# Layer 0 of a two-layer attention kernel: transposes in step 3 and in score tiles, other products at the ends of steps, moments over two steps

## The chip, the cores and the metric

The kernel runs on one core of one Trainium2 chip. A core has five engines that run side by side, each working through its own list of instructions in order, and telling each other of progress through semaphores: TensorE (PE; its weight loads are listed apart as PEld), VectorE (DVE), ScalarE (ACT), GpSimd (POOL) and SyncE (SP), which here issues all DMA transfers. PE writes its results to PSUM, DVE and ACT take them from there to SBUF, the working memory[...].

The metric is the device time of one execution in microseconds (us), lower is better. Before the change it was 3759.24 us, the median of three runs (3758.98 to 3764.71).

## The reference

The input x has 128 rows (S) of 256 positions (I) with 256 channels (C), all in float32. Two residual layers follow each other, each with a group norm in front:

```python
# layer 0: attention over the positions of a row, 8 heads of 32 channels, pair bias, gate
m_norm = layer_norm(m, ln_m_w, ln_m_b)          # m = _gn(x)
q = (m_norm @ Wq.T); k = (m_norm @ Wk.T); v = (m_norm @ Wv.T)      # split into 8 heads
b = (layer_norm(z) @ Wb.T)                       # a bias for each head, position and position
gate = sigmoid(m @ Wg.T + bg)
p = softmax(q @ k.T / sqrt(32) + b)
x = x + ((p @ v) * gate) @ Wo.T + bo
# layer 1: attention with 4 heads of 64 channels within a band of 16 positions
q, k, v = split(_gn(x) @ w_in.T + b_in)
x = x + softmax(band(q @ k.T / sqrt(64))) @ v @ w_out.T + b_out
```

Only the order of work in layer 0 is touched by the change; what is computed stays the same.

## The kernel before

The kernel has a part ahead of layer 0 (it makes the exponentials of the pair bias, `eb`, and the group moments of x), layer 0 and layer 1. Rows are worked on in pairs (class `Pair`); there are 64 pairs (`NP`), and a pair's input tile `xt` holds two rows as four blocks of 128 positions (`NT` = 4, `NB` = 2 blocks a row), 512 positions in all (`N2`). Channels are cut into two chunks of 128 (`KC` = 2).

For a pair, these methods run in turn. `Pair()` loads `xt` by DMA. `centre` and `scale` (POOL) make the group-normed `xg`. `moments` (DVE) gives each position's variance: four `bn_stats`, four `bn_aggr` and an addition. `root` raises it to the power -1/2 on POOL, and then two DMAs bring it from one value for each partition (`lrs`) to a row that stands in every partition: L1188 writes `rs_d` in memory, L1190 reads it back as `rs_r`, 128 copies of 512 values. `residual` (POOL) adds the output bias to `xt`. `turn` transposes `xg` on PE, four blocks for each chunk; of each result DVE makes `xnT`, multiplied with `rs_r` (L1200), and ACT the plain copy `xgT` (L1201). `project` makes qT and kT from `xnT` and gT from `xgT`, one chunk at a time; ACT takes the result from PSUM. `values(r)` and `keep_values(r)` make v of row r on PE and take it over with DVE.

Then there are four half steps of attention, for row r and chunk c (four heads): `scores(r, c)` on PE into two PSUM tiles, exponentials on ACT; `add_bias` multiplies one half with `eb` on DVE, the other on POOL; one step later `apply` multiplies the exponentials with v and with ones; `invert` takes reciprocals of the sums (DVE), `gate` multiplies with the gate (DVE, two instructions); `out_row` and `keep_row` multiply with Wo and add to the residual. `some(n)` issues up to n of the small DVE instructions that gather the moments for layer 1.

The order is written out by hand (`tc.manual_schedule()`): every engine's list follows the order of the calls. Each pair is four steps, each beginning with a call of `scores`, and in them stands work of four pairs: `was` (the one before), `now`, `nxt` (the next) and `nn` (the one after it). In each step PE's list begins with `scores` and `apply`; what comes after them on PE is:

| Step | scores | PE after scores and apply, before the change | after the change |
|---|---|---|---|
| 1 | now (0,0) | qT 1, kT 1, values 0 | qT 1, kT 1, values 0 |
| 2 | now (0,1) | gT 0, out_row 1 of was | gT 0, out_row 1 of was |
| 3 | now (1,0) | gT 1, values 1 | gT 1, turn of nxt, values 1 |
| 4 | now (1,1) | turn of nxt, out_row 0, qT 0 and kT 0 of nxt | qT 0 and kT 0 of nxt, out_row 0 |

[...] Layer 0 divides them into three pools: `ps_mm`, two tiles of one bank (tag `mm`: transposes, projections, values, output products), `ps_s`, two tiles of two banks (tag `s`: scores; one call of `scores` takes both), and `ps_o`, two tiles of one bank (results of `apply`). A tile is handed out again when its last reader is done. `xgT` and `xnT` have one buffer each in SBUF (`bufs=1`); a tile without `bufs` in the pool `sb` has two.

Of the kernel before, what the change touches and what calls it, by code (L numbers as in the profile page):

```python
# [9 lines left out]
F32 = mybir.dt.float32  # L10
AF = mybir.ActivationFunctionType
ALU = mybir.AluOpType
# [4 lines left out]
P = 128  # L17
# [756 lines left out]
def fast_kernel(  # L774
# [25 lines left out]
    nc = tc.nc  # L800
# [7 lines left out]
    NB = I // P  # L808
    KC = C // P
    NP = S // 2  # L810
    N2 = 2 * I
# [7 lines left out]
    ident = const.tile([P, P], F32, name="ident")  # L819
# [157 lines left out]
    with tc.tile_pool(name="pre", bufs=2) as pre, tc.tile_pool(  # L977
        name="pre1", bufs=1
# [5 lines left out]
        for w, dst in ((wq, qb), (wk, kb)):  # L984
            for m in range(KC):
                ps = pps.tile([P, 512], F32, name="b_ps", tag="mm")
# [7 lines left out]
        ps = pps.tile([P, 512], F32, name="b_ps", tag="mm")  # L994
# [5 lines left out]
        ps = pps.tile([P, 512], F32, name="b_ps", tag="mm")  # L1000
# [9 lines left out]
        for w in (wq, wk, wv):  # L1010
            ps = pps.tile([P, 512], F32, name="b_ps", tag="mm")
# [11 lines left out]
        ps = pps.tile([P, 512], F32, name="b_ps", tag="mm")  # L1023
# [117 lines left out]
    NT = 2 * NB  # L1141
# [5 lines left out]
    with tc.tile_pool(name="l0", bufs=2) as sb, tc.tile_pool(  # L1147
        name="l0s", bufs=4
    ) as sm, tc.tile_pool(name="ps_mm", bufs=2, space=PSUM) as ps_mm, tc.tile_pool(
        name="ps_s", bufs=2, space=PSUM  # L1150
    ) as ps_s, tc.tile_pool(name="ps_o", bufs=2, space=PSUM) as ps_o:

        def mm(name):
            return ps_mm.tile([P, 512], F32, name=name, tag="mm")

        class Pair:
# [15 lines left out]
            def residual(self):  # L1172
                nc.gpsimd.tensor_tensor(self.xt, self.xt, bcast(bo_r, 1, NT), ALU.add)

            def moments(self):
                st = sm.tile([P, NT, 6], F32, name="lst", tag="lst")
                self.mv = sm.tile([P, NT, 2], F32, name="lmv", tag="lmv")
                for t in range(NT):
                    nc.vector.bn_stats(st[:, t, :], self.xg[:, t, :])
                for t in range(NT):  # L1180
                    nc.vector.bn_aggr(self.mv[:, t, :], st[:, t, :])
                self.rs = sm.tile([P, NT], F32, name="lrs", tag="lrs")
                nc.vector.tensor_scalar_add(self.rs, self.mv[:, :, 1], 1e-5)

# [7 lines left out]

            def turn(self):
                self.xgT = sb.tile([P, KC, N2], F32, name="xgT", tag="xgT", bufs=1)
                self.xnT = sb.tile([P, KC, N2], F32, name="xnT", tag="xnT", bufs=1)
                for k in range(KC):
                    ps = mm("ps_x")
                    for t in range(NT):
                        nc.tensor.transpose(ps[:, t * P : (t + 1) * P], self.xg[:, t, k * P : (k + 1) * P], ident)
                    nc.vector.tensor_tensor(self.xnT[:, k, :], ps, self.rs_r, ALU.mult)  # L1200
                    nc.scalar.copy(self.xgT[:, k, :], ps)  # L1201

            def project(self, which, m):
                w, src, b, fn, sc = {
# [145 lines left out]
        def some(n):  # L1350
            for _ in range(min(n, len(later))):
                later.pop(0)()
# [10 lines left out]
        def pair(p):  # L1363
            return Pair(p) if p < NP else Nobody()

        now, nxt, nn = pair(0), pair(1), pair(2)
        for d in (now, nxt):
            d.centre()
            d.scale()
            if d is now:  # L1370
                d.moments()
                d.root()
            d.residual()
        now.turn()
# [3 lines left out]
        with tc.manual_schedule():  # L1378
            was, es, nn3 = Nobody(), None, None
            for p in range(NP):  # L1380

                e = now.scores(0, 0)
                now.add_bias(0, 0, e)
                nn.centre()
                was.apply(1, 1, es)
                was.invert(1, 1)
                was.gate(1, 1)
                now.project("qT", 1)
                now.project("kT", 1)
                nxt.moments()  # L1390
                some(1)
                now.values(0)
                now.keep_values(0)
                es = e

                nxt.root()
                e = now.scores(0, 1)
                now.add_bias(0, 1, e)
                nn.scale()
                now.apply(0, 0, es)  # L1400
                now.invert(0, 0)
                now.project("gT", 0)
                was.out_row(1)
                some(1)
                was.keep_row(1)
                now.gate(0, 0)
                es = e

                nn3 = pair(p + 3)
                e = now.scores(1, 0)  # L1410
                now.add_bias(1, 0, e)
                nn.residual()
                now.apply(0, 1, es)
                now.invert(0, 1)
                now.project("gT", 1)
                some(1)
                now.values(1)
                now.keep_values(1)
                now.gate(0, 1)
                es = e  # L1420

                e = now.scores(1, 1)
                now.add_bias(1, 1, e)
                now.apply(1, 0, es)
                nxt.turn()
                now.invert(1, 0)
                now.out_row(0)
                now.keep_row(0)
                now.gate(1, 0)
                nxt.project("qT", 0)  # L1430
                nxt.project("kT", 0)
                some(2)
                es = e
                was, now, nxt, nn = now, nxt, nn, nn3
            was.apply(1, 1, es)
            was.invert(1, 1)
            was.gate(1, 1)
            was.out_row(1)
            was.keep_row(1)
            some(len(later))  # L1440
# [26 lines left out]
    with tc.tile_pool(name="l1", bufs=2) as sb, tc.tile_pool(  # L1467
        name="l1s", bufs=4
    ) as sm, tc.tile_pool(name="ps1_mm", bufs=2, space=PSUM) as ps_mm, tc.tile_pool(
        name="ps1_s", bufs=1, space=PSUM  # L1470
    ) as ps_s, tc.tile_pool(name="ps1_o", bufs=1, space=PSUM) as ps_o:

        def mm1(name):
            return ps_mm.tile([P, 512], F32, name=name, tag="mm")
# [4 lines left out]
        for k in range(KC):  # L1479
            ps = mm1("ps_mr")  # L1480
# [137 lines left out]
        d = {}  # L1618
        for _ in prep1(0, d):
            pass  # L1620
        for p in range(NP):
            nxt = {}
# [16 lines left out]
            d = nxt  # L1639
# [5 lines left out]
    with tc.tile_pool(name="chk", bufs=1) as ck, tc.tile_pool(name="chk_ps", bufs=1, space=PSUM) as cps:  # L1645
        check(eb.rearrange("p h b i -> p (h b i)"), math.exp(-20.0), math.exp(20.0), 0, ck)
        for j, src in enumerate((rsum.rearrange("n q r c i -> (n q r c i)"), rsum1.rearrange("n q r i -> (n q r i)"))):
            t = ck.tile([P, src.shape[0] // P], F32, name=f"rs_all{j}")
            nc.sync.dma_start(t, src.rearrange("(a b) -> a b", a=P))
            check(t, 1e-16, 1e8, 1 + j, ck)  # L1650
        t = ck.tile([S, I], F32, name="mask_all")
# [4 lines left out]
        ps = cps.tile([P, 512], F32, name="ok_ps")  # L1656
# [4 lines left out]
@with_exitstack  # L1661
def mixer_kernel(ctx, tc, *args):

    nc = tc.nc
    keep = ctx.enter_context(tc.tile_pool(name="verdict", bufs=1))
    verdict = keep.tile([1, 1], mybir.dt.int32, name="verdict")
    fast_kernel(tc, *args, verdict)
    again = nc.values_load(verdict[0:1, 0:1], min_val=0, max_val=1)
    with tc.If(again > 0):
        general_kernel(tc, *args)  # L1670
# [53 lines left out]
```

## Time and profile before

| What | Value |
|---|---|
| Median of three runs | 3759.24 us |
| The profiled execution | 3762.96 us |
| Its span, from the first to the last instruction | 3761.2 us |
| PE busy | 3442.4 us (92%) |
| DVE busy | 2299.2 us (61%) |
| POOL busy | 1665.5 us (44%) |
| ACT busy | 1380.4 us (37%) |
| Mean granted PE clock | 0.974 |
| PE busy from 300 to 2380 us (the loop of layer 0) | 1961.13 us of 2080 |

The span is that of one profiled execution, from which all durations in the prediction come; the difference to the runs' median is some 2 us. PE's matmuls are pipelined and their ends are modelled, so that a busy PE isn't a PE at its peak. The profile names, for every idle time of an engine, what ended it; a wait is written as "engine tile line <- engine tile line". In the profile's names `ps_x` are the transposes' results, `ps_p` projections, `ps_v` values, `ps_y` output products, `ps_sc` scores, `ps_ov` results of `apply`. "SPq" is SP's DMA queue: an issue stands there with the time of the issue, not of the landing.

### The profile page before, as it was taken

The numbers are of one execution on the slowest core, as the hardware profiler recorded it, in microseconds if no ns is written. First come the engines' busy times: TensorE is split into PE (matmuls) and PEld (weight loads), VectorE is DVE, ScalarE is ACT, GpSimd is POOL, SyncE is SP. The second block draws the span as 40 slices with busy tenths as digits, with TensorE's granted clock in tenths as the row PEclk, the third lists the DMA queues.
The fourth block names the chain that finished last, engine by engine and source line by source line (L and its number), as shares of the span: only waits on it lengthen the run. The fifth ranks groups of instructions, "written<-read, shape, count | busy, mean of one in ns | idle before, by whom it ended". The sixth has DMA issues, their size and how long they took to land. (4 is left out here: it accounts for less than half of the span.)

```text
span 3761.2 us, 83462 instructions
## 1 busy us (share of the span) xinstructions
PE 3442.4 (92%) x37202; PEld 2102.0 (56%) x37202; DVE 2299.2 (61%) x3599; ACT 1380.4 (37%) x1937; POOL 1665.5 (44%) x873
## 2 busy tenths in 40 slices
PE   5657999999999999999999999799999999999996
PEld 3333555555555555555555555466666666666664
DVE  5864776777777777777777777544444444444446
ACT  2333343434343434333334343233333333333331
POOL 2354555555555555555555555322323323323321
PEclk8778999999999999999999999899999999999998
DMA  9950111111111111111111011111111111111111
GB/s 284 318 159 21 49 27 44 46 27 49 49 49 27 49 43 24 49 49 49 27 49 49 22 46 43 54 47 53 58 48 57 58 47 58 56 50 58 53 47 49
DMA packets 232994, 229.73 MB, mean 61 GB/s; under 512 B 41136, under 2 KB 207024, under 8 KB 232496
## 3 DMA queue, kind: packets, MB, share of 16 engines
q1 hardware_dynamic: 232624, 224.30, 20.2%
q8 instruction: 293, 4.80, 0.8%
q14 instruction: 77, 0.63, 0.1%
HBM read 155.46 MB, written 68.81 MB: 60 GB/s over the span
## 5 line engine op out<-in xcount | busy, mean ns | idle before, releaser
L1264 POOL TENSOR_TENSOR e<-e,eb 128x1024 f32<-128x1024 f32 x256 | 634.9, 2480 | 957.0 <-ACT e L1256 955.2
L1256 ACT ACTIVATE e<-ps_sc 128x1024 f32<-128x1024 f32 x512 | 496.6, 1022 | 479.2 <-PE ps_sc L1247 479.2
L1264 DVE TENSOR_TENSOR e<-e,eb 128x1024 f32<-128x1024 f32 x256 | 315.4, 1232 | 381.4 <-ACT e L1256 370.6
L1507 PE MATMUL ps_p<-xgT,w_in 128*128 128x512 f32 x1024 | 501.0, 613 | 4.4 <-ACT xgT L1499 0.4
L1556 POOL TENSOR_TENSOR e<-e,bw 128x384 f32<-128x384 f32 x256 | 250.6, 1000 | 477.1 <-ACT e L1554 477.1
L1283 DVE RECIPROCAL rv<-ps_ov 128x256 f32<-128x256 f32 x256 | 448.0, 1750 | 8.2 <-PE ps_ov L1274 6.4
L1247 PE MATMUL ps_sc<-qT,kT 32*128 32x256 f32 x4096 | 293.3, 400 | 49.8 <-ACT kT L1217 49.8
L1492 POOL TENSOR_TENSOR xb<-xt,bout_r 128x1024 f32<-128x1024 f32 x64 | 150.4, 2352 | 423.5 <-DVE yo L1595 419.0
L1308 PE MATMUL ps_y<-wo,oT 128*128 128x256 f32 x1024 | 250.3, 387 | 68.9 <-ACT xgT L1201 66.7
L1525 DVE TENSOR_TENSOR v<-ps_v,bv_r 128x512 f32<-128x512 f32 x128 | 84.5, 660 | 363.0 <-PE ps_v L1521 363.0
L1582 DVE TENSOR_TENSOR odd<-ps_o,odd 128x512 f32<-128x512 f32 x128 | 88.5, 692 | 340.3 <-ACT odd L1579 340.3
L1247 PEld LDWEIGHTS ps_sc<-qT,kT 32*128 32x128 f32 x4096 | 184.9, 184 | 172.5 <-ACT kT L1217 102.8
L1274 PE MATMUL ps_ov<-e,v 128*32 128x256 f32 x4096 | 274.7, 385 | 1.6 <-DVE v L1234 1.3
L1507 PEld LDWEIGHTS ps_p<-xgT,w_in 128*128 128x128 f32 x1024 | 179.1, 189 | 163.5 <-issue 107.1
L1213 PE MATMUL ps_p<-xnT,wq 128*128 128x512 f32 x512 | 249.2, 609 | 21.5 <-ACT xgT L1201 21.5
L1274 PE MATMUL ps_ov<-e,ones 128*32 128x256 f32 x4096 | 268.3, 379 | 0.0
L1308 PEld LDWEIGHTS ps_y<-wo,oT 128*128 128x128 f32 x1024 | 189.9, 190 | 135.1 <-ACT xgT L1201 81.6
L1213 PE MATMUL ps_p<-xgT,wg 128*128 128x512 f32 x512 | 253.9, 618 | 0.0
L1521 PE MATMUL ps_v<-w_in,xgT 128*128 128x256 f32 x1024 | 248.3, 385 | 0.0
L1591 PE MATMUL ps_y<-w_out,oT 128*128 128x256 f32 x1024 | 243.8, 381 | 2.6 <-DVE oT L1584 2.6
L1228 PE MATMUL ps_v<-wv,xnT 128*128 128x256 f32 x1024 | 241.9, 379 | 0.0
L1213 PE MATMUL ps_p<-xnT,wk 128*128 128x512 f32 x512 | 240.9, 593 | 0.0
(157 smaller groups left out, 5241.3 us busy)
## 6 DMA issues: line engine op xcount, KB each, us to landing
xa<-in_x_dram SPq DMA_DIRECT2D x8, 4096.0 KB
xt<-in_x_dram SPq DMA_DIRECT2D x64, 512.0 KB
x<-xo SPq DMA_DIRECT2D x16, 2048.0 KB
xt<-x SPq DMA_DIRECT2D x64, 512.0 KB
out_dram<-yo SPq DMA_DIRECT2D x64, 512.0 KB
rs_r<-rs_d SPq DMA_DIRECT2D x64, 256.0 KB
rs_d<-lrs SPq DMA_DIRECT2D x64, 2.0 KB
rsum<-rv SPq DMA_DIRECT2D x64, 16.0 KB
```

The source lines that it names most:

```text
L1213: nc.tensor.matmul(ps, w[:, k, m * P : (m + 1) * P], getattr(self, src)[:, k, :], start=(k == 0), stop=(k == KC - 1),)
L1228: nc.tensor.matmul(self.ps_v[:, b * C : (b + 1) * C], self.xnT[:, k, t * P : (t + 1) * P], wv[:, k, :], start=(k == 0), stop=(k == KC - 1),)
L1247: nc.tensor.matmul(self.pss[q // 2][:, q % 2, b, :], self.kT[rs, c, r * I + b * P : r * I + (b + 1) * P], self.qT[rs, c, r * I : (r + 1) * I],
L1256: nc.scalar.activation(e, self.pss[a], AF.Exp)
L1264: eng.tensor_tensor(es[a], es[a], eb[:, h : h + 2], ALU.mult)
L1274: nc.tensor.matmul(o[q * D0 : (q + 1) * D0, what, :], w, es[q // 2][:, q % 2, b, :], start=(b == 0), stop=(b == NB - 1),)
L1283: nc.vector.reciprocal(self.rv[:, r, c, :], self.o[:, 1, :])
L1308: nc.tensor.matmul(self.ps_y[:, b * C : (b + 1) * C], self.oT[:, k, b * P : (b + 1) * P], wo[:, k, :], start=(k == 0), stop=(k == KC - 1),)
L1507: nc.tensor.matmul(ps, w_in[:, k, n * C + m * P : n * C + (m + 1) * P], xgT[:, k, :], start=(k == 0), stop=(k == KC - 1),)
L1521: nc.tensor.matmul(ps[:, b * C : (b + 1) * C], xgT[:, k, t * P : (t + 1) * P], w_in[:, k, 2 * C : 3 * C], start=(k == 0), stop=(k == KC - 1),)
L1556: nc.gpsimd.tensor_tensor(e[:, q], e[:, q], bcast(bw.rearrange("p b w -> p (b w)"), 1, KC), ALU.mult)
L1591: nc.tensor.matmul(ps[:, b * C : (b + 1) * C], oT[:, k, b * P : (b + 1) * P], w_out[:, k, :], start=(k == 0), stop=(k == KC - 1),)
```

## The change

Four things change, all in layer 0:

- `turn` takes one score tile (tag `s`, two banks) for the transposes of both chunks, where it took two tiles of tag `mm`; and `xnT` gets two buffers.
- The loop calls `nxt.turn()` in step 3, after the gate projection, where it was in step 4 after `apply`.
- Step 4 has `qT 0` and `kT 0` of the next pair before `out_row(0)`; `keep_row(0)` and `gate(1, 0)` follow it. In step 3 `gate(0, 1)` comes before `values(1)`. Calls of `some` move within their steps.
- `moments` becomes `moments(0)`, two of the four `bn_stats`, which is called in step 4 for the pair after next, and `moments(1)`, the rest, in step 1.

```diff
-            def moments(self):
-                st = sm.tile([P, NT, 6], F32, name="lst", tag="lst")
-                self.mv = sm.tile([P, NT, 2], F32, name="lmv", tag="lmv")
+            def moments(self, r):
+                if r == 0:
+                    self.st = sm.tile([P, NT, 6], F32, name="lst", tag="lst")
+                    self.mv = sm.tile([P, NT, 2], F32, name="lmv", tag="lmv")
+                for t in range(r * NB, (r + 1) * NB):
+                    nc.vector.bn_stats(self.st[:, t, :], self.xg[:, t, :])
+                if r == 0:
+                    return
                 for t in range(NT):
-                    nc.vector.bn_stats(st[:, t, :], self.xg[:, t, :])
-                for t in range(NT):
-                    nc.vector.bn_aggr(self.mv[:, t, :], st[:, t, :])
+                    nc.vector.bn_aggr(self.mv[:, t, :], self.st[:, t, :])
...
-                self.xnT = sb.tile([P, KC, N2], F32, name="xnT", tag="xnT", bufs=1)
+                self.xnT = sb.tile([P, KC, N2], F32, name="xnT", tag="xnT")
+                pss = ps_s.tile([P, KC, N2], F32, name="ps_x", tag="s")
                 for k in range(KC):
-                    ps = mm("ps_x")
                     for t in range(NT):
-                        nc.tensor.transpose(ps[:, t * P : (t + 1) * P], self.xg[:, t, k * P : (k + 1) * P], ident)
-                    nc.vector.tensor_tensor(self.xnT[:, k, :], ps, self.rs_r, ALU.mult)
-                    nc.scalar.copy(self.xgT[:, k, :], ps)
+                        nc.tensor.transpose(
+                            pss[:, k, t * P : (t + 1) * P], self.xg[:, t, k * P : (k + 1) * P], ident
+                        )
+                    nc.vector.tensor_tensor(self.xnT[:, k, :], pss[:, k, :], self.rs_r, ALU.mult)
+                    nc.scalar.copy(self.xgT[:, k, :], pss[:, k, :])
...
         for d in (now, nxt):
             d.centre()
             d.scale()
+            d.moments(0)
             if d is now:
-                d.moments()
+                d.moments(1)
...
-                nxt.moments()
-                some(1)
+                nxt.moments(1)
                 now.values(0)
                 now.keep_values(0)
+                some(1)
...
                 now.project("gT", 1)
-                some(1)
+                nxt.turn()
+                now.gate(0, 1)
                 now.values(1)
                 now.keep_values(1)
-                now.gate(0, 1)
+                some(1)
...
                 now.apply(1, 0, es)
-                nxt.turn()
                 now.invert(1, 0)
+                nxt.project("qT", 0)
+                nxt.project("kT", 0)
+                nn.moments(0)
+                some(2)
                 now.out_row(0)
                 now.keep_row(0)
                 now.gate(1, 0)
-                nxt.project("qT", 0)
-                nxt.project("kT", 0)
-                some(2)
```

## The prediction

> **What bounds the kernel now.** I read the page, then the waits of TensorE (PE), then the timeline of one pair in the middle of layer 0, then the DMA queue (SP) and the granted clock. Layer 0 repeats every 32.72 us: its first scores of a pair start at 1191.08 and at 1223.80, and 63 of the 64 pairs turn a next pair. Inside the pair PE is busy without a hole except at two places, which the waits of PE between 310 and 2390 us name (columns: total us, times, longest):
>
> ```profile
> PE ps_y L1308 <- ACT xgT L1201: 66.7, 63, 3.2
> PE ps_sc L1247 <- ACT kT L1217: 49.0, 63, 0.8
> ```
>
> Together 115.7 us, 1.8 us a pair: all that better covering can win. Both are in step 4, as its timeline shows (start, duration, then what it waited for in brackets):
>
> ```profile
> 1215.48 1.09 PE L1199 MATMUL ps_x<-ident,xg 128*128 128x128 f32 x8
> 1216.18 1.29 DVE L1200 TENSOR_TENSOR xnT<-ps_x,rs_r 128x512 f32<-128x512 f32 x2 [0.17 <-PE ps_x L1199]
> 1216.95 1.13 ACT L1201 COPY xgT<-ps_x 128x512 f32<-128x512 f32 x2 [1.29 <-DVE xnT L1200]
> 1217.59 1.99 PE L1308 MATMUL ps_y<-wo,oT 128*128 128x256 f32 x8 [1.02 <-ACT xgT L1201]
> 1223.80 1.15 PE L1247 MATMUL ps_sc<-qT,kT 32*128 32x256 f32 x16 [0.78 <-ACT kT L1217]
> ```
>
> The output product wants one of the two PSUM buffers that the transposes hold; the next scores want the kT that was produced last. But turn also needs rs_r, the reciprocal deviations, which go through memory. Their road starts on POOL, behind a bias product and centre:
>
> ```profile
> 1194.28 2.48 POOL L1264 TENSOR_TENSOR e<-e,eb 128x1024 f32<-128x1024 f32 x1 [8.77 <-ACT e L1256]
> 1196.72 2.54 POOL L1167 TENSOR_TENSOR xg<-xt,M_l 128x1024 f32<-128x1024 f32 x1
> 1199.37 1.02 POOL L1187 TENSOR_TENSOR lrs<-lrs,mhalf 128x4 f32<-128x4 f32 x1
> ```
>
> and goes on in SP's queue, where the second issue waits for the first transfer:
>
> ```profile
> 1200.41 0.35 SPq L1188 DMA_DIRECT2D rs_d<-lrs  x1
> 1209.36 0.33 SPq L1190 DMA_DIRECT2D rs_r<-rs_d  x1
> ```
>
> The load's bytes move in these stretches (last columns: clock, DMA share, GB/s):
>
> ```profile
> 1212.15:1213.75 1.60, 1.60 (x23) 0.91 (x25) 1.10 (x2) 0.03 (x1) 1.60 (x1) 1.00 0.89 128
> 1213.75:1216.25 2.50, 2.50 (x39) 1.57 (x36) 2.21 (x4) 1.91 (x2) 0.71 (x2) 1.00 0.77 233
> ```
>
> rs_r is 256 KB (page, part 6); at 128 and 233 GB/s these cannot all have moved before 1214.0, and xnT ran at 1216.18 without waiting for it. The trace's completion marks of this transfer end at 1215.11. Over the loop those marks give 15.6 us from the start of the power on POOL to the landing (median; 15.0 to 16.0 for the middle eight tenths), against 16.8 until xnT: only 1.2 us of slack. Twice among the early pairs it ran out, which shows the landing directly, 16.1 and 15.8 us after the issue of rs_d (SP queue, then DVE):
>
> ```profile
> 316.54 0.36 SPq L1188 DMA_DIRECT2D rs_d<-lrs  x1
> ...
> 332.63 1.29 DVE L1200 TENSOR_TENSOR xnT<-ps_x,rs_r 128x512 f32<-128x512 f32 x2 [2.92 <-DMA rs_r<-rs_d]
> ...
> 480.60 0.35 SPq L1188 DMA_DIRECT2D rs_d<-lrs  x1
> ...
> 496.39 1.29 DVE L1200 TENSOR_TENSOR xnT<-ps_x,rs_r 128x512 f32<-128x512 f32 x2 [0.36 <-DMA rs_r<-rs_d]
> ```
>
> Last, the granted clock in windows of 3.41 us (first columns after the length: PE, PEld, DVE, ACT, POOL busy):
>
> ```profile
> 175.51:178.92 3.41, 1.56 (x9) 0.42 (x4) 0.58 (x3) 0.58 (x1) 0.57 (x1) 1.00 1.07 302
> 178.92:182.33 3.41, 0.00 (x0) 0.00 (x0) 0.00 (x0) 0.00 (x0) 3.41 (x1) 0.50 1.05 288
> 243.77:247.18 3.41, 0.02 (x1) 0.05 (x1) 3.41 (x11) 0.00 (x0) 3.41 (x1) 1.00 0.69 187
> 247.18:250.60 3.42, 3.42 (x16) 3.21 (x16) 3.32 (x14) 1.74 (x3) 3.42 (x2) 0.50 0.00 0
> 329.10:332.52 3.42, 1.70 (x24) 0.99 (x12) 0.61 (x1) 0.00 (x0) 2.82 (x1) 1.00 0.66 153
> 332.52:335.93 3.41, 1.88 (x9) 1.68 (x10) 2.96 (x3) 1.13 (x2) 0.00 (x0) 1.00 0.20 70
> ```
>
> A window in which PE was busy for 1.56 us or less is followed by one at half clock, one with 1.70 us is not. So about 1.8 us of idleness inside one window costs the next window half its speed.
>
> [...] rs_d is 512 elements of 4 bytes for 2 KB and keeps rs_r back by 8.95 us. [...]
>
> **The change, part by part.** Times are counted from the first scores of a pair (0). Before, steps take 8.30, 6.58, 6.58 and 11.26 us (scores at 1191.08, 1199.38, 1205.96, 1212.54, 1223.80).
>
> Order at the ends of steps (costed together): step 4 now ends in the output product. kT is ready 1.8 us earlier for the next scores, and the output product no longer needs a transpose's buffer. Both holes go: -1.8 us. Steps would be 8.30, 6.58, 6.58 + 1.09 (transposes) = 7.67, and 11.26 - 1.80 - 1.09 = 8.37: 30.9 us. In step 1 keep_row and gate now spill over from step 4; 0.69 + 0.42 + 0.42 from 0.2 end at 1.75, before DVE's bias product at 2.24, so nothing.
>
> Moments in two: two statistics leave step 1, 0.7 us of DVE. Their result used to be ready (1199.29) just as POOL ended centre (1199.26), and POOL's chain is not touched: bias product from 3.20, centre from 5.64 to 8.18. The power starts at 8.2 instead of 8.29. I take a gain of 0.1; if POOL did not bind it would be 0.7.
>
> xnT with two buffers: lets values(1) read the old one while the new is written; free.
>
> turn in step 3. It reaches PE at 14.88 + 4.76 = 19.6 (scores, apply, gate projection as in 1205.96 to 1210.72). DVE has its first transposes and is done with the reciprocal at 20.4. rs_r lands at 8.2 + 15.6 = 23.8, its issues stand on SP's queue as before (rs_d, rs_r, xt), and nothing in their way moves. So DVE stops for 3.4 us, with gate(0,1), keep_values(1) and the bias product behind it. Before, the same wait had 1.2 us to spare; turn is now 4.8 us earlier relative to the power.
>
> One PSUM tile for both chunks: before, each chunk had its own. In the built program the second multiplication waits for the first copy and the second copy for the second multiplication, though they are in different banks. So eviction is a chain: 0.69 + 0.57 + 0.69 + 0.57 and three hand-overs of 0.08 (1216.87 to 1216.95) = 2.75 us instead of 1.9. It ends at 23.9 + 2.75 = 26.65.
>
> Score tiles: turn takes one of two, so of scores(1,1) only the first two matmuls can run at 22.55; the third waits for the last copy. PE stands from about 23.0 to 26.7: 3.7 us. Then 0.9 of scores remain. apply(1,0) needs v: 23.9 + 2.1 (to the end of the second multiplication) + 0.42 + 0.42 + 0.69 = 27.5, PE is there at 27.6: no more. The rest of the step is as step 1 after its scores: 8.30 - 1.08 = 7.2. Pair: 26.7 + 0.9 + 7.2 = 34.8 us, 2.1 more than before.
>
> Clock: a hole of 3.7 us always puts over 1.8 us into one window, so every pair has at least one half-clock window. Averaged over where the hole falls: started in the first 0.3 of a window it costs some 1.4 us (rest of the next window at half speed), from 0.3 to 1.6 some 2.7 (that rest and a full window, since a window at half clock with 2.57 us busy, 73.11 to 76.52, did not bring the clock back), later 1.7 (a full window). Weighted 2.0 us, bounds 0 and 3.0. PE has nothing else to hide it behind in step 4. I take 2.0: 36.8 us, 4.15 more a pair.
>
> Sum: 63 x 4.15 = +261 us on 3761.2 = 4022 of span. The median of the runs stands 2 us below that span, so 4020. The prologue's turn changes by 1 us at most; layer 1 is not touched.
>
> **Rivals.** (A) The wait for rs_r comes, the clock does not fall, because partial windows or waiting matmuls count otherwise: 63 x 2.1 = +135, 3895. For it: only pre-loop windows show the threshold; against: all of these agree. (B) The other side: rs_r is in time. Then the hole is only the eviction chain (20.5 + 2.75 = 23.3 against 23.0, 0.3) and v (gate under POOL's load 0.97, so 24.6 against 24.2, 0.4 more): 30.9 + 0.9 with hand-overs = 31.8, -0.9 a pair, 3702. It decides if power to landing falls under 12.2 us; no pair of before is under 14.9. (C) The trip shortens by some 2 us, the hole stays under 1.8 and eats the gain: 3760. (D) The hole mostly meets the costly part of the window or is over 4 us: 5.2 a pair, 4085 and above.
>
> **How the numbers follow.** Forecast 0.58, A 0.17, B 0.07, C 0.03, D 0.15. The range is 3880 to 4110: it holds the forecast's own 3960 to 4080, A, and most of D; B and C are left out. A run of this kernel tells 0.2% (7.5 us) from no change. Faster is B, 0.07; same is C, 0.03; slower 0.90.
>
> **What would show it.** Right: DVE xnT waits for DMA rs_r some 63 times, about 3.4 us each; PE scores wait for ACT xgT about 3.7 us each; ps_y waits for xgT and scores for kT are gone; PEclk in the middle slices is below 9; the power on POOL starts 8.2 us after a pair's scores. Wrong: xnT waits for PE or for the copies instead; scores wait under 1.5 us; PEclk stays at 9 (A).

## The result, and the profile after

The changed kernel takes 4078.8 us (median of four runs, 4072.0 to 4083.5) against 3761.6 us for the one before (four runs): a ratio of 1.084 (95% interval 1.082 to 1.086), 317 us more. The forecast was 4020, with a range of 3880 to 4110.

From the page of the changed kernel, the first line of part 1 and the lines of busy share and clock in part 2:

```profile
span 4080.0 us, 83402 instructions
PE 3550.1 (87%) x37202; PEld 2181.5 (53%) x37202; DVE 2317.0 (57%) x3599; ACT 1383.8 (34%) x1937; POOL 1664.3 (41%) x873
...
PE   5648888888888888888888888879999999999996
...
PEclk8769989999999989998999999989999999999998
```

The loop of layer 0 is where PE shows 8 in place of 9 and where the clock falls below 9 here and there; the slices of layer 1 are as before. Over the loop (300 to 2700 us) the mean granted clock is 0.94, which in tenths still shows as 9 in most slices; so the prediction's sign "PEclk below 9" came only in some, and this line could not decide on rival A. The waits of PE and of DVE in the loop (310 to 2700 us; total us, times, longest):

```profile
PE ps_x L1202 <- ACT xgT L1206: 328.5, 63, 10.1
```

```profile
DVE xnT L1205 <- DMA rs_r<-rs_d: 240.4, 63, 5.6
...
DVE xnT L1205 <- PE ps_x L1202: 119.3, 63, 2.3
```

The two waits of PE before the change, 115.7 us, are gone. One has come in their place, 5.2 us a pair, and it is not at the scores: PE stands ahead of transposes (`ps_x`), until ACT has copied `xgT`. The timeline of one pair in the changed kernel shows who waits for whom (start, duration, instruction, in brackets what it waited for):

```profile
1302.97 1.02 POOL L1190 TENSOR_TENSOR lrs<-lrs,mhalf 128x4 f32<-128x4 f32 x1
...
1304.01 0.36 SPq L1191 DMA_DIRECT2D rs_d<-lrs  x1
...
1312.60 0.33 SPq L1193 DMA_DIRECT2D rs_r<-rs_d  x1
...
1314.34 0.60 PE L1202 MATMUL ps_x<-ident,xg 128*128 128x128 f32 x4
...
1318.80 0.69 DVE L1205 TENSOR_TENSOR xnT<-ps_x,rs_r 128x512 f32<-128x512 f32 x1 [4.09 <-DMA rs_r<-rs_d]
1319.58 0.59 ACT L1206 COPY xgT<-ps_x 128x512 f32<-128x512 f32 x1 [4.36 <-DVE xnT L1205]
1320.22 1.12 PE L1202 MATMUL ps_x<-ident,xg 128*128 128x128 f32 x4 [5.28 <-ACT xgT L1206]
1321.13 3.01 PE L1233 MATMUL ps_v<-wv,xnT 128*128 128x256 f32 x8
1321.44 0.69 DVE L1205 TENSOR_TENSOR xnT<-ps_x,rs_r 128x512 f32<-128x512 f32 x1 [1.95 <-PE ps_x L1202]
...
1324.07 1.15 PE L1252 MATMUL ps_sc<-qT,kT 32*128 32x256 f32 x16
```

Read from the top: the power on POOL starts at 1302.97, 8.3 us after this pair's first scores at 1294.70; rs_r lands 15.7 us later, and DVE, which had been waiting for 4.09 us, multiplies the first chunk; ACT copies it; only then does PE transpose the second chunk, after 5.28 us of standing. Then its four transposes and the values follow, slowed: the transposes take 1.12 us where those of the first chunk took 0.60, the values 3.01 where those of the kernel before take 1.89 (at 1210.72 in its timeline). The granted clock of the same stretch, in its own windows of 3.41 us (busy time of PE, PEld, DVE, ACT, POOL, then clock, DMA share, GB/s):

```profile
1316.56:1319.97 3.41, 0.00 (x0) 0.00 (x0) 0.69 (x1) 0.39 (x1) 0.98 (x1) 1.00 0.62 211
1319.97:1323.39 3.42, 3.17 (x10) 2.73 (x11) 1.45 (x3) 0.78 (x2) 0.00 (x0) 0.50 0.00 0
1323.39:1326.80 3.41, 3.41 (x52) 1.98 (x50) 1.52 (x3) 1.55 (x2) 0.00 (x0) 1.00 0.00 0
```

Here a window without work on PE is followed by one at half clock (0.50), in which the work after the hole falls. A pair takes 37.7 us now (the same scores at 1302.99 and at 1340.66), 5.0 more than before; on average it takes 37.8 (from the first scores of pair 1 at 308.48 to those of pair 64 at 2689.47).

### The profile page after: what moved, and what is told of

It reads as the page before. It is cut to its first block, busy times and chain, and to the rows that moved or that the text cites. A ratio compares the mean times of both kernels' runs of the same rounds, so it can differ in the third digit from the quotient of the medians.

```text
span 4080.0 us, 83402 instructions
## 1 busy us (share of the span) xinstructions
PE 3550.1 (87%) x37202; PEld 2181.5 (53%) x37202; DVE 2317.0 (57%) x3599; ACT 1383.8 (34%) x1937; POOL 1664.3 (41%) x873
## 5 line engine op out<-in xcount | busy, mean ns | idle before, releaser
L1202 PE MATMUL ps_x<-ident,xg 128*128 128x128 f32 x512 | 106.3, 345 | 346.5 <-ACT xgT L1206 328.5
L1233 PE MATMUL ps_v<-wv,xnT 128*128 128x256 f32 x1024 | 327.8, 478 | 0.0
L1205 DVE TENSOR_TENSOR xnT<-ps_x,rs_r 128x512 f32<-128x512 f32 x128 | 88.5, 692 | 377.1 <-DMA rs_r<-rs_d 254.7
L1233 PEld LDWEIGHTS ps_v<-wv,xnT 128*128 128x128 f32 x1024 | 253.3, 255 | 73.2 <-issue 31.1
L1202 PEld LDWEIGHTS ps_x<-ident,xg 128*128 128x128 f32 x512 | 74.8, 173 | 396.1 <-ACT xgT L1206 343.9
```

The source lines that it names most:

```text
L1202: nc.tensor.transpose(pss[:, k, t * P : (t + 1) * P], self.xg[:, t, k * P : (k + 1) * P], ident)
L1233: nc.tensor.matmul(self.ps_v[:, b * C : (b + 1) * C], self.xnT[:, k, t * P : (t + 1) * P], wv[:, k, :], start=(k == 0), stop=(k == KC - 1),)
```

## The experiments

Theory W: rs_r lands too late for a turn in step 3, the wait stops TensorE through the chain of evictions, and the hole costs clock. Rival C: the chain through the one PSUM tile makes the hole, whenever rs_r comes. Rival O: the new order of the step ends costs. (These letters are not those of the prediction's rivals.) Times of experiments are single runs unless a number of runs is given; the kernel before ran beside each group (3761.5, 3761.8 and 3759.9 us).

**The wait taken away by other data** (e1_const_row). This kernel leaves out the scaling by the deviations.

```diff
+    one_row = const.tile([P, NT * P], F32, name="one_row")
+    nc.vector.memset(one_row, 1.0)
...
-                    nc.vector.tensor_tensor(self.xnT[:, k, :], pss[:, k, :], self.rs_r, ALU.mult)
+                    nc.vector.tensor_tensor(self.xnT[:, k, :], pss[:, k, :], one_row, ALU.mult)
```

> The changed kernel, but xnT is multiplied with a tile of ones that is made once, not with rs_r; the power, both DMAs and all the order stay, so the scaling by the deviation is left out of q, k and v and only the wait for the landing goes. Theory W (the late landing makes the hole): DVE starts the first product at 20.4 us after a pair's scores instead of 24.1; the second transposes still wait for product and copy of the first chunk, 0.7 + 0.1 + 0.6 + 0.1, so a hole of about 1.6 us is left, too short for the clock to fall each time. Pair 32.5 us, time about 3750 (3720 to 3790), PEclk 9 in the loop. Rival C (the chain through the one PSUM tile makes the hole, rs_r or not): a hole of over 4 us stays and the time stays above 4000. Rival O (the new order of the step ends costs): above 3850.

Measured: 3723.3 us. PE waits 1.5 us a pair for the second transposes (310 to 2600 us):

```profile
PE ps_x L1204 <- ACT xgT L1208: 96.2, 63, 4.3
```

The clock is 1.00 over the loop (0.975 over the whole run); only three windows of 3.41 us in it, near its start, are at half speed. C and O fall: the same tile, the same chain and the same order, without the wait, are faster than the kernel before. The time is 27 us under the expectation. A pair of 32.4 us on average in place of 32.5 is some 7 us of that, and most of the rest lies ahead of the loop, where the first turn has no landing to wait for either: the second pair's power starts at 299.0 us here, at 316.4 in the changed kernel.

**The wait taken away by an earlier start** (e4_early_root). Nothing is left out here.

```diff
-                nxt.moments(1)
...
-                nxt.root()
...
                 nn.moments(0)
+                nn.moments(1)
+                nn.root()
```

(The two calls stand in the prologue for both first pairs as well.)

> The changed kernel, but all moments and the power with its two DMAs are issued in step 4 for the pair after next, some 10 us before step 1's place; nothing is left out. Theory W: the landing comes long before turn; DVE does not wait for rs_r; what is left is the chain of the first chunk, a hole of about 1.6 us: pair 32.5, time about 3750 (3720 to 3790). Rival C: still above 4000. Rival O: above 3850.

Measured: 3738.3 us. Its timeline at turn:

```profile
1329.90 0.60 PE L1202 MATMUL ps_x<-ident,xg 128*128 128x128 f32 x4
1330.54 0.69 DVE L1205 TENSOR_TENSOR xnT<-ps_x,rs_r 128x512 f32<-128x512 f32 x1 [0.27 <-PE ps_x L1202]
1331.32 0.59 ACT L1206 COPY xgT<-ps_x 128x512 f32<-128x512 f32 x1 [0.53 <-DVE xnT L1205]
1331.96 0.66 PE L1202 MATMUL ps_x<-ident,xg 128*128 128x128 f32 x4 [1.46 <-ACT xgT L1206]
```

The product follows the transposes at once; what remains is the chain of one chunk, 1.46 us, and these 63 holes (94.7 us together) cost next to no clock: only one window of the loop, at 329.64, is at half speed, and the mean over the run is 0.974, as in the kernel before beside it. A pair is 32.3 us, the same as with the row of ones. So without the lateness of rs_r the loss is gone, and issuing the power earlier takes the lateness away.

**A tile for each chunk** (e2_two_tiles).

```diff
-                pss = ps_s.tile([P, KC, N2], F32, name="ps_x", tag="s")
                 for k in range(KC):
+                    pss = ps_s.tile([P, KC, N2], F32, name="ps_x", tag="s")
```

(and `pss[:, 0, ...]` for `pss[:, k, ...]`.)

> The changed kernel, but each chunk's transposes have a score tile of their own, so that the second transposes wait for nothing of the first chunk. Theory W: DVE still waits for rs_r, some 3.5 to 4 us a pair; the second transposes and values run in that time, and the hole moves to the scores of step 4, where it is about 2.8 us instead of 5.3, with a fall of the clock in most pairs, 1.4 us. Pair 35 to 35.5, time about 3930 (3890 to 3970). Rival C: with the chain gone the pair falls to about 31 us and the time to about 3650 to 3700.

Measured: 3858.8 us. PE no longer waits at the transposes, but at the scores, in its waits from 310 to 2500 us:

```profile
PE ps_sc L1252 <- ACT xgT L1206: 120.8, 63, 6.2
```

That is 1.9 us a pair. DVE still waits for rs_r, 162.9 us in 57 of the pairs, 2.9 us each. The hole is smaller than expected by 0.9 and the time by 70 us; in this run rs_r took 14.4 us from the power to the landing, not 15.6 (median, from the completion marks of the trace), which the expectation did not know. Beside a_again below, on which the same road takes 14.4 us too, the two tiles alone are worth 192 us. So the chain is a part of the loss; with the landing in time it costs only the 1.46 us a pair of e4_early_root.

The expectation foresaw that the clock would fall, and it does: PE runs at half speed for 2.5 us a pair, and the mean over the run is 0.954. Two windows of this kernel (columns as above):

```profile
944.28:947.69 3.41, 1.94 (x19) 1.19 (x17) 2.71 (x6) 1.13 (x3) 1.08 (x1) 1.00 0.51 160
947.69:951.10 3.41, 3.41 (x32) 1.38 (x32) 1.49 (x2) 1.93 (x2) 1.40 (x1) 0.50 0.00 0
```

In the first PE was busy for 1.94 us and idle for 1.47, and still the next is at half clock. The prediction had read from the windows ahead of the loop that 1.70 us of work keep the clock. That reading does not hold in general.

**The hole filled with idle work** (e3_filled, and e3_filled_b beside a_again).

```diff
+                    if k == 0 and fill:
+                        ps_f = mm("ps_f")
+                        for n in range(4):
+                            nc.tensor.matmul(ps_f, ident, w_in[:, 0, 0:512], start=(n == 0), stop=(n == 3))
```

> The changed kernel with four more matmuls (128x512, constants, nobody reads the result) on TensorE between the first and the second transposes, in the hole. They take some 3.6 us of the 5.3, so the same waits end at the same time, but no window is half idle any more. If the clock costs as theory W has it, the transposes and values after the hole run at full speed again: 1.5 us a pair less, time about 3985 (3960 to 4010), mean clock near 0.97. If the fall of the clock costs nothing (rival: what follows the hole is bound by something else), the time stays at 4080 or rises.

Measured: 3907.9 us, mean clock 0.975. Against the first measurement of the changed kernel that is 171 us less, more than the expected 95. But rs_r took 14.6 us here and 15.7 there, so the two are not comparable; the next two runs stand side by side.

**The changed kernel once more** (a_again), unedited.

> The changed kernel itself, unedited, on the chip of the three runs beside it, because the road of rs_r from the power to the landing took 15.7 us in its first profile and 14.4 to 14.6 in the four experiments before this. If that is the chip's or the moment's own, it shows again here, and by theory W every microsecond of it is one microsecond of each pair: pair 8.3 to the power + road + 0.1 + 1.45 for product and copy of the first chunk + 2.35 for transposes and values + 8.3 for step 4 + 1.5 to 2 for the clock. Road 14.5: pair 36.3 to 36.8, time 3985 to 4020. Road 15.7: 37.7, 4080. If the pair does not follow the road, W is wrong.

Measured: 4051.1 us, the pair 37.4 us on average, with a road (from the start of the power to the landing of rs_r) of 14.4 us. The expectation was 3985 to 4020: a road shorter by 1.3 us shortened the pair by 0.4 only. The hole did follow the road, from 5.2 us a pair to 4.1. What took the rest back is the clock: its mean over the run is 0.928, against 0.941 in the first profile, and half speed lasts 6.4 us a pair, against 4.5. So here W was wrong in its sum: the clock's price is not fixed. Of a_again, two windows:

```profile
1301.37:1304.78 3.41, 0.44 (x5) 0.20 (x2) 0.90 (x2) 0.69 (x1) 3.04 (x2) 1.00 0.47 152
1304.78:1308.19 3.41, 2.76 (x9) 2.40 (x10) 1.45 (x3) 1.17 (x2) 0.00 (x0) 0.50 0.22 78
```

```profile
1305.43 1.12 PE L1202 MATMUL ps_x<-ident,xg 128*128 128x128 f32 x4 [3.62 <-ACT xgT L1206]
```

This hole of 3.6 us left PE 0.44 us of work in the first window, and the next is at half clock.

> The kernel with the filled hole again (e3_filled), on the same chip as the unedited changed kernel, so that the price of the clock is read without the difference of the road. W: 1.5 to 2 us a pair less than the unedited one, 95 to 125 us in all. If the clock costs nothing: equal to it within 10 us.

Measured beside it: 3904.9 us, 146 us less, 2.3 us a pair, more than the expected 95 to 125. The timeline of this kernel shows the same wait for rs_r, with PE at work in it:

```profile
1310.44 0.60 PE L1202 MATMUL ps_x<-ident,xg 128*128 128x128 f32 x4
1310.88 3.60 PE L1210 MATMUL ps_f<-w_in,ident 128*128 128x512 f32 x8
1313.52 0.69 DVE L1205 TENSOR_TENSOR xnT<-ps_x,rs_r 128x512 f32<-128x512 f32 x1 [2.71 <-DMA rs_r<-rs_d]
1314.30 0.59 ACT L1206 COPY xgT<-ps_x 128x512 f32<-128x512 f32 x1 [2.97 <-DVE xnT L1205]
1314.94 0.66 PE L1202 MATMUL ps_x<-ident,xg 128*128 128x128 f32 x4 [0.46 <-ACT xgT L1206]
1315.43 1.89 PE L1237 MATMUL ps_v<-wv,xnT 128*128 128x256 f32 x8
```

Transposes take 0.66 us again and values 1.89: adding 252 useless matmuls makes the kernel 146 us faster, and the clock is 1.00 over the loop (300 to 2500 us), where that of a_again is 0.91 (300 to 2700 us). That is the clock's price, measured alone.

**The moments in one piece** (e7_onemom).

```diff
+                nxt.moments(0)
                 nxt.moments(1)
...
-                nn.moments(0)
```

> The changed kernel, but all four statistics of the moments stand in step 1 again, as before the change. W: POOL's chain sets the start of the power; DVE would have the moments some 0.1 to 0.7 us later than now and they come just when POOL is done or a little after; the time is that of the unedited changed kernel, or up to 0.7 us a pair (44 us) more. Rival M (the split of the moments is what delays): the time falls by more than 20 us.

Measured: 4059.2 us beside 4051.1; 8 us is within what the changed kernel's own runs differ by (4072 to 4083). The split neither gains nor loses what one run can tell. The traces say the same: the power starts 8.3 us after a pair's scores in both.

**turn in step 4 again** (e6_turn4).

```diff
                 now.project("gT", 1)
-                nxt.turn()
...
                 now.apply(1, 0, es)
+                nxt.turn()
                 now.invert(1, 0)
```

> The changed kernel, but turn stands in step 4 again, after apply and ahead of qT and kT; score tile, order of the ends and split moments stay. W: rs_r is needed at 25 us after a pair's scores and lands at 22.9 to 24, so DVE does not wait for it; two holes are left by the chain through the one tile, about 1.5 us before the second transposes and 0.9 before qT, none long enough for the clock: pair 33.4, time about 3800 (3770 to 3830). If the place of turn is not what matters, the time stays with the unedited changed kernel.

Measured: 3853.7 us. The place of turn is what matters (197 us less than the unedited kernel beside it, and no wait for rs_r is left), but 3800 was expected. The waits of PE in this kernel name what was missed:

```profile
PE ps_ov L1279 <- DVE v L1239: 102.7, 62, 2.6
PE ps_x L1202 <- ACT xgT L1206: 91.9, 63, 1.7
```

and its timelines of DVE and of POOL why v was late:

```profile
1318.50 2.58 DVE L1295 SCALAR_TENSOR_TENSOR gr<-gT,rv 128x256 f32<-128x256 f32 x1 [0.55 <-ACT gT L1222]
...
1321.45 0.68 DVE L1239 TENSOR_TENSOR v<-ps_v,vb_r 128x512 f32<-128x512 f32 x1
```

```profile
1318.45 2.34 POOL L1173 TENSOR_TENSOR xt<-xt,bo_r 128x1024 f32<-128x1024 f32 x1
```

The change put gate(0,1) ahead of values(1). There its first instruction starts when POOL has just begun `residual` (1318.45 to 1320.79) and ends at 1321.08, after 2.58 us; it took 0.41 in the changed kernel (at 1322.05), where POOL was idle from 1317.55 to 1327.27.

**The same with values first** (e8_turn4_v).

> As e6_turn4, but values(1) and its copy stand ahead of gate(0,1) again, as before the change. e6_turn4 came out at 34.2 us a pair instead of the expected 33.4: apply(1,0) waited 1.64 us for v, which stood on VectorE behind a gate instruction of 2.58 us that took 0.97 in the kernel before. If the order of gate and values is the cause, this hole goes: pair 32.6 to 32.9, time 3750 to 3770. If v is late for another reason, the time stays near 3854.

Measured: 3748.7 us, 105 us less than e6_turn4 (1.67 us a pair): about as expected. So the order of gate and values was a loss of its own, waiting behind the larger one; in the changed kernel it is hidden, because POOL is done with `residual` (at 1317.55) by the time rs_r lets DVE reach gate (at 1322.05).

**All three mended** (e5_early_two): the early root, a tile for each chunk, values(1) ahead of gate(0,1).

> The changed kernel with three edits: all moments and the power with its DMAs in step 4 for the pair after next (as e4_early_root), a score tile for each chunk's transposes (as e2_two_tiles), and values(1) with its copy ahead of gate(0,1). W: neither rs_r nor the chain of the first chunk makes TensorE wait; both chunks are out of PSUM by 22.5 us after a pair's scores, when the scores of step 4 want the tiles. Pair 31 us, the sum of its steps; time about 3655 (3640 to 3690), faster than both kernels. If another wait stands behind these two, it shows above 3700.

Measured: 3631.5 us (median of four runs, 3631.2 to 3633.3), ratio to the kernel before 0.966 (95% interval 0.964 to 0.968). It is faster than both kernels. Its timeline at turn:

```profile
1307.13 1.04 PE L1202 MATMUL ps_x<-ident,xg 128*128 128x128 f32 x8
1307.77 1.29 DVE L1205 TENSOR_TENSOR xnT<-ps_x,rs_r 128x512 f32<-128x512 f32 x2 [0.27 <-PE ps_x L1202]
1308.00 1.89 PE L1233 MATMUL ps_v<-wv,xnT 128*128 128x256 f32 x8
1308.55 1.13 ACT L1206 COPY xgT<-ps_x 128x512 f32<-128x512 f32 x2 [0.53 <-DVE xnT L1205]
1309.82 1.15 PE L1252 MATMUL ps_sc<-qT,kT 32*128 32x256 f32 x16
```

No instruction of PE waits here, and a pair takes 30.6 us on average, 2.1 less than before. It came out 24 us under the expectation. Against e4_early_root the two further edits gain 107 us, 1.7 a pair; the chain's 1.5 is gone, and what each edit gives here was not separated.

## Why the prediction was right

The whole of it, as measured beside the experiments: 4051 - 3762 = 289 us. Taking it apart in order: the clock 146 us (a_again to e3_filled_b), the late landing 167 us (e3_filled_b to e4_early_root, across two groups of runs), and what the new order gains, -23 us (e4_early_root against its own kernel before). The shares depend on what is taken away first: the early power alone gives 313 us, the two tiles alone 192, since each also shortens the hole that costs clock (1.5 and 1.9 us a pair in place of the 4.1 of a_again).

- **Order at the ends of steps, -1.8 us a pair.** Right: both waits are gone in every kernel with the new order. The gain shows whole only in e5_early_two; in e4_early_root 1.46 us of it are eaten by the chain.
- **Moments in two, nothing.** Right: the power starts 8.3 us after a pair's scores, behind `centre` as foreseen (predicted 8.2), and e7_onemom shows no difference. The two statistics that DVE saves in step 1 do not even let it finish earlier: its last instruction for the moments (L1186) took 0.17 us in the kernel before and takes 0.81 here, from 1302.08, and ends 0.03 us after `centre` on POOL (1300.33 to 1302.86). What holds it back was not tested.
- **The wait for rs_r.** Right in place, cause and size: 63 waits, 240.4 us, 3.8 each; 3.4 were predicted.
- **One PSUM tile for both chunks.** This is the step that failed. The prediction saw the chain between DVE and ACT, but let PE write the second chunk's transposes and values while the first chunk was waiting, so that PE would stand at the scores for 3.7 us. In the built program the second transposes wait as well, for the first copy, since both chunks are one tile. The hole is 5.2 us on average (328.5 in 63), and transposes and values (0.5 and 1.8) come after it, not in it. By the trace a pair without the clock's loss is 8.3 + 15.7 + 0.1 + 1.45 (product, copy, hand-overs) + 2.35 (transposes and values) + 8.3 (step 4) = 36.2 us, not 34.8. The same sum gives 35.0 for e3_filled_b, with its road of 14.55, and its pairs take 35.0. e2_two_tiles built what the prediction had assumed, and there the hole is at the scores.
- **The clock, 2.0 us a pair.** Right as a mechanism, which no wait shows: measured alone it is 2.3 us; in the first profile, by the sum above, 37.7 - 36.2 = 1.5. The limit on which it rested, the author's estimate of some 1.8 us of idleness in a window, did not hold: 1.47 were enough in e2_two_tiles, and in the changed kernel a window with 1.48 us of work (1425.80 to 1429.21) kept the clock, while the prediction's lines had shown a fall at 1.56.
- **The sum.** 4.15 us a pair were predicted (its own numbers, 36.8 - 32.72, give 4.1), 5.0 measured. The missed position of the hole is +1.2 of the difference, a landing 0.2 us later than predicted (24.0 after the scores in place of 23.8) +0.2, the clock -0.5. That two errors offset each other is luck: with the clock's 2.0 as predicted, the longer hole would have given some 4110 us (4078.8 + 63 x 0.5), the end of the range.

Rival D came nearer to the time than the forecast: a hole over 4 us, 5.2 us a pair, 4085 and above; measured are a hole of 5.2, 5.1 us a pair on average, and 4078.8. What made the hole that long, the second transposes waiting behind the first copy, it did not name. Rival A (no fall of the clock) is refuted by the windows and by e3_filled_b, rival B (rs_r in time) by 63 waits. B's own sum, 31.8 us a pair if rs_r came in time, missed the same step: e4_early_root measured 32.3.

## What to carry to other kernels

Before an instruction is moved forward, look up for each of its inputs how long before use it arrives: rs_r, waited for only three times in the loop of the kernel before (3.5 us in all), had 1.2 us to spare, and as its transfer still started where its producer stood, moving the consumer alone turned that slack into 63 waits of 3.8 us. The tile that was written and read in two chunks was one tile to those who waited (63 waits, 328.5 us); with a tile for each chunk (e2_two_tiles) no wait at the transposes was left, so give parts that should overlap a tile each. And ask of a hole on TensorE not only how long it is, but whether the clock falls after it: holes of 1.5 us ahead of transposes cost next to none here (e4_early_root), while holes of 1.9 us ahead of scores (e2_two_tiles) and of 4 to 5 us did.

## What the runs showed of the hardware

- Filling a hole with matmuls that nobody reads gained 146 us (a_again to e3_filled_b). After a window with PE busy for 0.44 us of 3.41 the next one was at half clock, and after 2.76 us of work in that one the clock was full again (a_again, 1304.78 to 1308.19; full at 1308.19).
- The busy time of PE alone did not say whether the clock falls. After 1.94 us of work in a window it fell in e2_two_tiles, after 1.48 it did not in the changed kernel. The hole of e2_two_tiles is followed by scores (matmuls of 32 x 128, by their form in the timeline), that of e4_early_root by transposes (128 x 128); whether this makes the difference was not tested.
- The road from the power to the landing of rs_r, the same two transfers in the same order, took 15.6 and 15.7 us (medians) in the first profiles of the two kernels and 14.2 to 14.6 in all ten experiments; one of these, a_again, is the changed kernel itself. Both transfers were shorter: from the first issue to the second 8.5 us in a_again, 9.1 in the first profile of the changed kernel; from the second issue to the landing 4.7 and 5.3. Why stays open.
- A shorter road did not shorten the pair in proportion (1.3 us against 0.4), because the pairs ran at half speed for 4.5 us each in the first profile and for 6.4 in a_again. Why the shorter hole cost more clock was not tested.
- The first gate instruction (`gr`, with gT and rv as inputs) took 0.41, 0.97 or 2.58 us, by how much of a running POOL instruction was left when it started; where it was held up, it ended 0.3 us after that one (1321.08 after 1320.79 in e6_turn4, and 1214.23 after 1213.95 in the kernel before). In the changed kernel 125 of its 256 executions began beside a running POOL instruction; they took 0.79 to 2.64 us and ended 0.27 to 0.29 us after it. The other 131 took 0.41 to 0.43. Why it waits was not shown. The prediction took 0.97 from the old place of gate; what it cost in these runs followed from when POOL's instruction ended.
